# Row sums of the softmax from pairs of key tiles, and an fp16 low-rank product, in a layer of two MoE-LoRA half steps around causal attention

## The chip, the cores and the metric

The kernel runs on one core of a Trainium2 chip. The metric is the device time of one execution in microseconds (us); lower is better. The core has five engines with a queue each, served in order: TensorE (PE, matmuls; its weight loads are listed apart as PEld), VectorE (DVE), ScalarE (ACT), GpSimd (POOL) and SyncE (SP, which here only issues DMAs). Engines wait for each other through semaphores.

## What is computed

```python
x = x + 0.5 * ffn(layernorm(x))
x = x + attention(layernorm(x))
x = x + 0.5 * ffn(layernorm(x))

# ffn: 8 experts, top 2, rank 16
logits = x @ gate_w.T
w      = softmax over the two largest logits, 0 elsewhere
low    = x @ lora_A.T                     # per expert, 8 x 16 = 128 values
y      = x @ base_w.T + base_b + 2.0 * sum over experts of w * (low @ lora_B.T)

# attention: 32 query heads, 8 key-value heads, head size 32, causal, rotary
att   = (q @ k.T) / sqrt(32), masked
probs = softmax(att)
out   = (probs @ v) @ Wo
```

x has 2 x 1024 rows of 1024 values, all in fp32.

## The kernel before, in words

**Tiles.** The 2048 rows are 16 tiles of 128 rows, eight in each of the two batches (TPB = 8). A tile passes four stages: a1 (layernorm, first ffn), a2 (layernorm, keys, values and queries), the attention proper, c1 (output matrix) and c2 (layernorm, second ffn, store). A planner written out by hand (NORMAL, SEQS, plan, step, lines 807 to 939) mixes pieces of the dense stages of later and earlier tiles into the attention units of the current tile. The framework then orders the instructions of each engine by a timeline of its own, so that a change in one place can redraw the order elsewhere.

**Precision.** Large products are made of fp16 halves: each operand is scaled by a power of two (pow2, line 167, which squares and sums the weights on ACT, spreads the largest row sum with a small matmul and takes a power of two from it), a high half is its fp16 rounding and a low half the rest (split, line 195). A dense product is three fp16 matmuls for each 128 of the contraction (lines 361 to 363: high x high, high x low, low x high), 512 columns wide.

**The ffn** (lines 393 to 447). The gate and low-rank products of a tile come first (136 columns); then the eight experts' weights are made on DVE and ACT and multiplied into the 128 low-rank values, with the factor inva2 that undoes the scale of lora_A (line 418). After the base product of each half (512 columns) three more matmuls add the low-rank part into the same PSUM tile (lines 441 to 443). Their operands, lh, ll and lbh, lbl, are halves in fp32r, a form of fp32. lora_B therefore is scaled by the scale of the base weights alone (prep_lora, line 226). L444 then adds the result to x.

**Attention** (lines 556 to 696). A unit is one query tile and one key-value group of four query heads; with L key tiles in reach (1 to 8), there are 128 units and 576 pairs of a unit and a key tile. unit_s1 finds the row maxima: for each key tile four matmuls into one of two PSUM buffers (L568), and a maximum on DVE (L585). Where L > 2, the diagonal tile goes through ACT (L579) and a select on POOL (L580) first. The maxima are written into two spare columns of the queries, which are transposed by a DMA (qt_load, line 549). LOOK lets this run 3 to 6 units ahead. unit_s2 then makes the scores with the key on the partitions (L683, one matmul of 512 columns), and the exponentials on ACT (L689, tile p32, 8 buffers); in the diagonal tile POOL sets what is masked to 0 (L691).

**The weighted sum** (av_batch, line 615). Up to four key tiles (BATCH) of one unit wait in pend, and a batch is issued when two more key tiles (SKEW) have been made. For each key tile, last one first, PE multiplies the exponentials with the values and then with a matrix of ones; the ones product gives the row sums, spread over the 32 rows of a head. Both are fp32 matmuls with 32 columns of weights and 128 columns of data, one for each of the four heads, placed in four column groups of the array. The matmuls of a batch are held in a row. At the end of a unit ACT copies both results out (L637), DVE takes the reciprocal of the sums and multiplies (L639, L644), and ACT and POOL write the fp16 halves for the output product (L645, L646).

**The start** (lines 741 to 799). SP issues the loads in program order while pinned is set: x of tile 0, the gate's and lora_A's weights, two pieces of the base weights, x of tile 1, then two more pieces, lora_B (lst, line 758), x of tile 2. prep_gate, prep_base and prep_lora scale and split them.

Of the kernel before, what the change touches and what calls it, by code (L numbers as in the profile page):

```python
# [9 lines left out]
FP = mybir.dt.float32  # L10
FPR = mybir.dt.float32r
HP = mybir.dt.float16
I32 = mybir.dt.int32
AF = mybir.ActivationFunctionType
ALU = mybir.AluOpType
# [5 lines left out]
P = 128  # L21
# [19 lines left out]
def kernel(  # L41
# [77 lines left out]
    def pin(ins):  # L119

        if pinned[0]:
            tc.keep_in_program_order(ins)
# [12 lines left out]
    ag = wres.tile([P, 2, KB, P + E], HP)  # L135
    lbh = wres.tile([P, D], FPR)
    lbl = wres.tile([P, D], FPR)
    wstr = dram.tile([5, 2, P, 2, KB // 2, 512], HP)
# [27 lines left out]

    def pow2(aps, junk, name):

# [11 lines left out]
        e = small.tile([P, 1], FP, name="e")  # L180
        nc.vector.tensor_scalar(e.bitcast(I32), ar.bitcast(I32), 0x7F800000, None, ALU.bitwise_and)
        tag = "_".join(map(str, name))
        s = const.tile([P, 1], FP, name="s_" + tag)
# [20 lines left out]
    def prep_base(n, sts):  # L204
        pow2(sts, [wb[:, n, 0, h * HK : (h + 1) * HK, :] for h in range(2)], ("b", n))
        for k in range(KB):
            after = (None, None)
            if n == 0 and k > 0:
                after = ("xn", "nb") if k == 1 else ("hi", "lo")
            split(wb[:, n, 0, k, :], wb[:, n, 1, k, :], sts[k // HK][:, k % HK, :], S["b", n], k, after)  # L210
        u = const.tile([P, 1], FP, name=f"uf{n}")
        nc.gpsimd.tensor_scalar(u, INV["b", n], 0.5 / XS, 0.0, ALU.mult, ALU.add)
        S["uf", n] = u

    def prep_gate(sts):
# [6 lines left out]
        inva2 = const.tile([P, 1], FP)  # L222
        nc.gpsimd.tensor_scalar(inva2, INV["a",], 2.0, 0.0, ALU.mult, ALU.add)
        S["cg"], S["inva2"] = cg, inva2
# [168 lines left out]
    def ffn(xt, tt, done):  # L393
# [32 lines left out]
        for n in range(2):  # L426
# [5 lines left out]
            if n == 0:  # L432
                pst = p_misc.tile([P, 512], FP, name="misc")
                nc.tensor.transpose(pst[:, 0:P], lw.rearrange("p e r -> p (e r)"), ident)
                lh = small.tile([P, P], FPR, name="lh", bufs=LB)
                ll = small.tile([P, P], FPR, name="ll", bufs=LB)
                nc.scalar.copy(lh, pst[:, 0:P])
                nc.vector.tensor_tensor(ll, pst[:, 0:P], lh.bitcast(FP), ALU.subtract)
                yield
# [175 lines left out]
    def av_batch():  # L615

        t, g, L, us = pend.popleft()
        if us[0][0] == 0:
            avt[0] = p_av.tile([P, 2, P], FP, name="av")
        av = avt[0]  # L620
        prev = None
        for n, (j, p32) in enumerate(reversed(us)):
            for i, w in enumerate((VA[t - t % TPB + j][:, g, :], ones)):
                for h in range(GRP):
                    rows = slice(h * DH, (h + 1) * DH)
                    with ExitStack() as st:
                        if prev is not None:
                            st.enter_context(tc.high_priority())
                            st.enter_context(tc.issue_after(prev.ins))
                        prev = nc.tensor.matmul(  # L630
                            av[rows, i, :], lhsT=w, rhs=p32[:, h, :],
                            start=(us[0][0] == 0 and n == 0 and i == 0), stop=(us[-1][0] == L - 1 and n == len(us) - 1),
                            skip_group_check=True, tile_position=(0, h * DH),
                        )
        if us[-1][0] == L - 1:
            o = pp.tile([P, 2, P], FP, name="o", bufs=2)
# [12 lines left out]

    def av_add(t, g, j, L, p32):  # L650

        if not pend or len(pend[-1][3]) == BATCH or pend[-1][0:2] != (t, g):
            pend.append((t, g, L, []))
        pend[-1][3].append((j, p32))
        after = 0
# [20 lines left out]
    def unit_s2(t, g):  # L676
# [4 lines left out]
        for j in range(L):  # L681
# [8 lines left out]
            if j == L - 1:  # L690
# [3 lines left out]
                )  # L694
            av_add(t, g, j, L, p32)
            yield
# [46 lines left out]
    for h in range(2):  # L743
        for src, c in ((a_in, slice(0, P)), (g_in, slice(P, P + E))):
# [258 lines left out]
```

## Time and profile before

| | |
|---|---|
| time, median of 3 runs | 1538.43 us (1531.92 to 1540.04) |
| time of the profiled execution | 1540.01 us |
| its span, first to last instruction | 1538.2 us |
| PE busy | 1434.5 us, 93% |
| DVE busy | 1080.9 us, 70% |
| ACT busy | 691.1 us, 45% |
| POOL busy | 480.0 us, 31% |
| row sums' matmuls (L630, ones) busy | 232.1 us |
| low-rank matmuls (L441, L442, L443) busy | 35.7, 25.7 and 26.8 us |
| chain that ended last, PE's share | 70% |

Busy time is the time in which at least one instruction of a group or engine runs; matmuls overlap, so their mean duration is longer than the distance from one to the next. An fp32 matmul leaves two records in the trace. A line such as "PE s L568 <- DVE mx L585" reads: the instruction of line 568, which writes tile s, waited for the one of line 585 on DVE, which writes mx; then come the total in us, the number of times and the longest.

### The profile page before, as it was taken

The page shows a single profiled execution, that of the slowest core. Times are in us where ns is not written, and L with a number is a line of the kernel's source. Part 1 is how long each engine was busy: PE and PEld are TensorE (multiplying, and loading weights), DVE is VectorE, ACT ScalarE, POOL GpSimd, SP SyncE. Part 2 cuts the span into 40 slices and gives each one's busy share as a digit, 9 for nine tenths or more (in the row PEclk, how much of TensorE's full clock was granted, in tenths as well). Part 3 has the DMA queues.
Part 4 walks back from the last instruction along what each step waited for, and adds up shares of the span by engine and source line. Part 5 has one row for each costly group of instructions (what it writes and reads, how often), then busy time and mean ns, then how long its engine had stood idle before and what let it go on. Part 6 is the DMA issues. An engine that isn't in the chain of part 4 may idle for free.

```text
span 1538.2 us, 39420 instructions
## 1 busy us (share of the span) xinstructions
PE 1434.5 (93%) x16594; PEld 846.2 (55%) x16594; DVE 1080.9 (70%) x2382; ACT 691.1 (45%) x1276; POOL 480.0 (31%) x678
## 2 busy tenths in 40 slices
PE   3687889899999999999999998999999999999997
PEld 2333445455656566666654454555656656666543
DVE  5968666958768577777664866867768577776553
ACT  7453334444444454454550334444445445555420
POOL 2544332524324133232131433433333232221221
PEclk9998999999999999999999999999999999999999
DMA  9776797969383763855647769566493753553551
GB/s 301 250 207 185 172 242 190 235 166 242 84 254 96 209 173 79 238 106 146 184 116 244 178 189 257 157 196 203 111 256 75 220 145 97 194 132 96 112 180 42
DMA packets 297186, 267.57 MB, mean 174 GB/s; under 512 B 262576, under 2 KB 265648, under 8 KB 276528
## 3 DMA queue, kind: packets, MB, share of 16 engines
q1 hardware_dynamic: 293456, 252.47, 61.5%
q10 hardware_dynamic: 3552, 12.58, 2.1%
q8 instruction: 130, 2.13, 0.6%
q14 instruction: 48, 0.39, 0.1%
HBM read 181.63 MB, written 20.45 MB: 131 GB/s over the span
## 4 chain that ended last, share of the span: by engine, by line
PE 70%; DVE 11%; DMA 10%; issue 3%; POOL 2%; ACT 2%; SPq 1%; ACTq 0%; DVEq 0%; POOLq 0%
PE av L630 14%; PE pd L361 12%; PE pd L362 12%; PE pd L363 12%; PE s L568 8%; PE s L683 7%; DMA qt<-qst 5%; DMA ws<-wstr 2%; DVE mx L585 2%; DVE hl L314 2%; DMA tt<-hl 2%; DVE rc L639 1%; PE pd L441 1%; PE pd L442 1%; PE pd L443 1%
## 5 line engine op out<-in xcount | busy, mean ns | idle before, releaser
L689 ACT ACTIVATE p<-s,cs 128x512 f32<-128x512 f32 x576 | 380.0, 688 | 279.4 <-PE s L683 276.2
L585 DVE TENSOR_REDUCE mx<-s 128x4 f32<-128x512 f32 x480 | 316.4, 676 | 182.0 <-PE s L568 155.9
L630 PE MATMUL av<-p,va 128*32 128x128 f32 x4608 | 236.6, 277 | 2.3 <-POOL p L691 1.3
L361 PE MATMUL pd<-ws,tt 128*128 128x512 f16 x592 | 225.4, 381 | 13.8 <-DMA ws<-wstr 9.4
L630 PE MATMUL av<-p,ones 128*32 128x128 f32 x4608 | 232.1, 273 | 0.0
L362 PE MATMUL pd<-ws,tt 128*128 128x512 f16 x592 | 225.2, 380 | 0.0
L363 PE MATMUL pd<-ws,tt 128*128 128x512 f16 x592 | 224.6, 380 | 0.0
L361 PEld LDWEIGHTS <-tt 128*128 128x128 f16 x1360 | 134.2, 99 | 163.3 <-DMA tt<-hl 28.1
L568 PE MATMUL s<-kts,qt 96*128 96x128 f16 x2304 | 200.0, 220 | 15.3 <-DMA qt<-qst 10.3
L361 PE MATMUL pd<-wb,tt 128*128 128x512 f16 x512 | 196.1, 383 | 17.2 <-DVE xt L444 11.7
L362 PEld LDWEIGHTS <-tt 128*128 128x128 f16 x1360 | 134.2, 99 | 140.4 <-issue 25.0
L683 PE MATMUL s<-qt,kts 128*128 128x512 f16 x576 | 201.9, 382 | 9.3 <-DMA qt<-qst 7.8
L568 PEld LDWEIGHTS <-qt 96*128 96x128 f16 x2304 | 149.9, 98 | 101.8 <-issue 37.7
L363 PEld LDWEIGHTS <-tt 128*128 128x128 f16 x1360 | 134.1, 99 | 129.3 <-issue 7.0
L362 PE MATMUL pd<-wb,tt 128*128 128x512 f16 x512 | 195.9, 383 | 2.2 <-DVE wb L202 2.2
L363 PE MATMUL pd<-wb,tt 128*128 128x512 f16 x512 | 195.7, 382 | 0.0
L630 PEld LDWEIGHTS av<-p,va 128*32 128x32 f32 x4608 | 122.4, 109 | 66.0 <-issue 54.8
L646 POOL TENSOR_TENSOR tt<-o,tt 128x128 f16<-128x128 f32 x128 | 62.7, 490 | 305.1 <-ACT tt L645 305.1
L691 POOL TENSOR_SCALAR_AFFINE_SELECT p<-p 128x512 f32<-128x512 f32 x128 | 85.9, 672 | 198.2 <-ACT p L689 197.1
L639 DVE RECIPROCAL rc<-o 128x128 f32<-128x128 f32 x128 | 121.0, 945 | 37.2 <-ACT o L637 36.9
L630 PEld LDWEIGHTS av<-p,ones 128*32 128x32 f32 x4608 | 138.2, 110 | 0.1
L580 POOL TENSOR_SCALAR_AFFINE_SELECT sm<-sm 128x512 f32<-128x512 f32 x96 | 67.8, 706 | 216.1 <-ACT sm L579 213.5
(164 smaller groups left out, 1815.6 us busy)
## 6 DMA issues: line engine op xcount, KB each, us to landing
ws<-wstr SPq DMA_DIRECT2D x148, 1024.0 KB, 5.9
wstr<-ws ACTq DMA_DIRECT2D x9, 1024.0 KB, 6.5
xt<-in_x_dram SPq DMA_DIRECT2D x16, 512.0 KB, 3.7
out_dram<-xt SPq DMA_DIRECT2D x15, 512.0 KB, 3.1
qt<-qst SPq DMA_TRANSPOSE x256, 3.0
ws<-in_wb_dram SPq DMA_DIRECT2D x2, 1024.0 KB, 8.4
qst<-in_wb_dram SPq DMA_DIRECT2D x2, 1024.0 KB, 7.9
st<-in_wo_dram SPq DMA_DIRECT2D x2, 1024.0 KB, 11.3
```

The costliest lines, as they stand in the source:

```text
L361: nc.tensor.matmul(ps, lhsT=th, rhs=wh, start=(k == 0), stop=False)
L362: nc.tensor.matmul(ps, lhsT=th, rhs=wl, start=False, stop=False)
L363: nc.tensor.matmul(ps, lhsT=tl, rhs=wh, start=False, stop=(last and k == KB - 1))
L568: nc.tensor.matmul(ps[:, h, :], lhsT=q[0 : 3 * DH, h, :], rhs=KT[b0 + j][0 : 3 * DH, g, :], start=(not pem or h == 0), stop=not pem,)
L580: nc.gpsimd.affine_select(out=sm, in_=sm, compare_op=ALU.is_ge, fill=-3.0e38, base=0, pattern=[[0, GRP], [-1, P]], channel_multiplier=1,)
L585: nc.vector.tensor_reduce(mx[:, j, :], ps, AX.X, ALU.max)
L630: prev = nc.tensor.matmul(av[rows, i, :], lhsT=w, rhs=p32[:, h, :], start=(us[0][0] == 0 and n == 0 and i == 0), stop=(us[-1][0] == L - 1 ...
L639: nc.vector.reciprocal(rc, o[:, 1, :])
L646: nc.gpsimd.tensor_tensor(c.low(g), o2, c.high(g), ALU.subtract)
L683: ins = nc.tensor.matmul(ps.rearrange("p h k -> p (h k)"), lhsT=KT[b0 + j][:, g, :], rhs=q.rearrange("p h k -> p (h k)"), start=True, stop ...
L689: nc.scalar.activation(p32, ps, AF.Exp, scale=cs)
L691: nc.gpsimd.affine_select(out=p32, in_=p32, compare_op=ALU.is_ge, fill=0.0, base=0, pattern=[[0, GRP], [1, P]], channel_multiplier=-1,)
```

## The change

Two parts.

First, the row sums: when a unit has made an odd-numbered key tile's exponentials, DVE adds them to those of the tile before (128x512, fp32, a new tile "pair" with 3 buffers), and PE multiplies the sum with ones, once for the pair. A last tile without a partner is multiplied by itself. In a batch, the value products of all its tiles come first and the ones products after them.

Second, the low-rank product: lbh, lbl, lh and ll become fp16. lora_B gets a power-of-two scale of its own, so it is loaded ahead of the base weights, and its sum of squares is taken right after the gate's. The scales of the base weights get a lower bound ("least"), inva2 is put together from three scales once the first base scale is known, and the factors of lora_B's two halves are made in prep_lora.

```diff
-    lbh = wres.tile([P, D], FPR)
-    lbl = wres.tile([P, D], FPR)
+    lbh = wres.tile([P, D], HP)
+    lbl = wres.tile([P, D], HP)
...
-    def pow2(aps, junk, name):
+    def pow2(aps, junk, name, least=None):
...
+        if least is not None:
+            nc.vector.tensor_tensor(e, e, least, ALU.max)
...
     def prep_base(n, sts):
-        pow2(sts, [wb[:, n, 0, h * HK : (h + 1) * HK, :] for h in range(2)], ("b", n))
+
+        least = const.tile([P, 1], FP, name=f"lb{n}")
+        if n == 0:
+            nc.vector.scalar_tensor_tensor(least, INV["a",], 2.0**32, INV["l",], ALU.mult, ALU.mult)
+        else:
+            nc.vector.tensor_scalar(least, INV["b", 0], 16384.0, None, ALU.mult)
+        pow2(sts, [wb[:, n, 0, h * HK : (h + 1) * HK, :] for h in range(2)], ("b", n), least)
+        if n == 0:
+            inva2 = const.tile([P, 1], FP)
+            nc.vector.scalar_tensor_tensor(inva2, INV["a",], 2.0, INV["l",], ALU.mult, ALU.mult)
+            nc.vector.tensor_tensor(inva2, inva2, S["b", 0], ALU.mult)
+            S["inva2"] = inva2
...
     def prep_lora(st):
+        c = const.tile([P, 2], FP, name="sl")
+        nc.vector.tensor_copy(c[:, 0:1], S["l",])
+        nc.vector.scalar_tensor_tensor(c[:, 1:2], INV["b", 0], S["l",], S["b", 1], ALU.mult, ALU.mult)
         for n in range(2):
-            c = bass.ts(n, 512)
-            nc.scalar.activation(lbh[:, c], st[:, c], AF.Copy, scale=S["b", n])
-            nc.vector.scalar_tensor_tensor(
-                lbl[:, c], st[:, c], S["b", n], lbh[:, c].bitcast(FP), ALU.mult, ALU.subtract
-            )
+            h, s = bass.ts(n, 512), c[:, n : n + 1]
+            nc.scalar.activation(lbh[:, h], st[:, h], AF.Copy, scale=s)
+            nc.vector.scalar_tensor_tensor(lbl[:, h], st[:, h], s, lbh[:, h], ALU.mult, ALU.subtract)
...
-                lh = small.tile([P, P], FPR, name="lh", bufs=LB)
-                ll = small.tile([P, P], FPR, name="ll", bufs=LB)
+                lh = small.tile([P, P], HP, name="lh", bufs=LB)
+                ll = small.tile([P, P], HP, name="ll", bufs=LB)
...
-        for n, (j, p32) in enumerate(reversed(us)):
-            for i, w in enumerate((VA[t - t % TPB + j][:, g, :], ones)):
-                for h in range(GRP):
...
+        last = us[-1][0] == L - 1
+        runs = [(0, VA[t - t % TPB + j][:, g, :], p32) for j, p32, _ in reversed(us)]
+        runs += [(1, ones, sums) for _, _, sums in reversed(us) if sums is not None]
         prev = None
+        for n, (i, w, p32) in enumerate(runs):
+            for h in range(GRP):
...
-            av_add(t, g, j, L, p32)
+            sums = None
+            if j % 2 == 1:
+                sums = pp.tile([P, GRP, P], FP, name="pair", bufs=3)
+                nc.vector.tensor_tensor(sums, even, p32, ALU.add)
+            elif j == L - 1:
+                sums = p32
+            even = p32
+            av_add(t, g, j, L, p32, sums)
             yield
...
+    lst = xp.tile([P, D], FP, name="xt")
+    pin(nc.sync.dma_start(out=lst, in_=lb_in))
     b0 = [piece(h - 2, [wb_in[:, 0:512]], h, nc.sync) for h in range(2)]
...
     prep_gate(gst)
+    pow2([lst[:, bass.ts(h, 512)] for h in range(2)], [lbh[:, bass.ts(h, 512)] for h in range(2)], ("l",))
     b1 = [piece(3 + h, [wb_in[:, 512:1024]], h, nc.sync) for h in range(2)]
-    lst = xp.tile([P, D], FP, name="xt")
-    pin(nc.sync.dma_start(out=lst, in_=lb_in))
```

More of the change, by code (lines that the diff above doesn't have):

```diff
@@ L10 @@
 FP = mybir.dt.float32
-FPR = mybir.dt.float32r
 HP = mybir.dt.float16
@@ L221, in prep_gate @@
         nc.gpsimd.tensor_scalar(cg, INV["a",], 1.0 / XS, 0.0, ALU.mult, ALU.add)
-        inva2 = const.tile([P, 1], FP)
-        nc.gpsimd.tensor_scalar(inva2, INV["a",], 2.0, 0.0, ALU.mult, ALU.add)
-        S["cg"], S["inva2"] = cg, inva2
+        S["cg"] = cg
     def prep_lora(st):
+        c = const.tile([P, 2], FP, name="sl")
+        nc.vector.tensor_copy(c[:, 0:1], S["l",])
+        nc.vector.scalar_tensor_tensor(c[:, 1:2], INV["b", 0], S["l",], S["b", 1], ALU.mult, ALU.mult)
         for n in range(2):
-            c = bass.ts(n, 512)
-            nc.scalar.activation(lbh[:, c], st[:, c], AF.Copy, scale=S["b", n])
-            nc.vector.scalar_tensor_tensor(
-                lbl[:, c], st[:, c], S["b", n], lbh[:, c].bitcast(FP), ALU.mult, ALU.subtract
-            )
+            h, s = bass.ts(n, 512), c[:, n : n + 1]
+            nc.scalar.activation(lbh[:, h], st[:, h], AF.Copy, scale=s)
+            nc.vector.scalar_tensor_tensor(lbl[:, h], st[:, h], s, lbh[:, h], ALU.mult, ALU.subtract)
         nc.scalar.mul(bb, bb, 0.5)
@@ L434, in ffn @@
                 nc.tensor.transpose(pst[:, 0:P], lw.rearrange("p e r -> p (e r)"), ident)
-                lh = small.tile([P, P], FPR, name="lh", bufs=LB)
-                ll = small.tile([P, P], FPR, name="ll", bufs=LB)
+                lh = small.tile([P, P], HP, name="lh", bufs=LB)
+                ll = small.tile([P, P], HP, name="ll", bufs=LB)
                 nc.scalar.copy(lh, pst[:, 0:P])
-                nc.vector.tensor_tensor(ll, pst[:, 0:P], lh.bitcast(FP), ALU.subtract)
+                nc.vector.tensor_tensor(ll, pst[:, 0:P], lh, ALU.subtract)
                 yield
@@ L620, in av_batch @@
         av = avt[0]
+        last = us[-1][0] == L - 1
+        runs = [(0, VA[t - t % TPB + j][:, g, :], p32) for j, p32, _ in reversed(us)]
+        runs += [(1, ones, sums) for _, _, sums in reversed(us) if sums is not None]
         prev = None
-        for n, (j, p32) in enumerate(reversed(us)):
-            for i, w in enumerate((VA[t - t % TPB + j][:, g, :], ones)):
-                for h in range(GRP):
[L625 to L635, printed above, removed]
+        for n, (i, w, p32) in enumerate(runs):
+            for h in range(GRP):
+                rows = slice(h * DH, (h + 1) * DH)
+                with ExitStack() as st:
+                    if prev is not None:
+                        st.enter_context(tc.high_priority())
+                        st.enter_context(tc.issue_after(prev.ins))
+                    prev = nc.tensor.matmul(
+                        av[rows, i, :], lhsT=w, rhs=p32[:, h, :],
+                        start=(us[0][0] == 0 and n == 0), stop=(last and n == len(runs) - 1),
+                        skip_group_check=True, tile_position=(0, h * DH),
+                    )
+        if last:
             o = pp.tile([P, 2, P], FP, name="o", bufs=2)
@@ L648, in av_batch, with av_add @@
                 CT[t] = CTX.pop(t)
-    def av_add(t, g, j, L, p32):
+    def av_add(t, g, j, L, p32, sums):
         if not pend or len(pend[-1][3]) == BATCH or pend[-1][0:2] != (t, g):
             pend.append((t, g, L, []))
-        pend[-1][3].append((j, p32))
+        pend[-1][3].append((j, p32, sums))
         after = 0
```

## The prediction

> **What bounds the kernel now.** I read the page's 40 slices first, then a table of windows, then the list of waits, the chain of work that ended last, and the groups of instructions by line.
>
> ```profile
> PE   3687889899999999999999998999999999999997
> DVE  5968666958768577777664866867768577776553
> ```
>
> TensorE (PE) is above 90% in nearly every slice from the tenth on, VectorE (DVE) at 6 to 8 tenths. Before about 300 us PE has holes; they belong to the preparation of the weights. The windows give the middle (stretch, length, then busy us and instructions of PE, its weight loads, DVE, ScalarE = ACT, GpSimd = POOL; clock, DMA share, GB/s):
>
> ```profile
> 300.00:400.00 100.00, 97.08 (x1188) 59.80 (x1188) 74.06 (x179) 47.01 (x94) 30.78 (x49) 1.00 0.72 176
> 400.00:500.00 100.00, 100.00 (x1235) 60.19 (x1233) 75.18 (x157) 46.36 (x86) 35.81 (x46) 1.00 0.59 163
> 600.00:700.00 100.00, 99.69 (x1355) 62.29 (x1355) 71.95 (x151) 49.71 (x90) 27.44 (x38) 1.00 0.62 161
> 1000.00:1100.00 100.00, 98.13 (x1115) 58.16 (x1113) 75.63 (x160) 45.31 (x86) 36.65 (x48) 1.00 0.61 168
> 1300.00:1400.00 100.00, 97.32 (x1501) 63.13 (x1500) 74.67 (x146) 56.30 (x102) 23.67 (x37) 1.00 0.58 172
> ```
>
> PE is full at full clock, and in the whole run it waits 2.8 us for DVE's row maxima, the one place in attention where DVE could hold it often:
>
> ```profile
> PE s L568 <- DVE mx L585: 2.8, 6, 0.8
> ```
>
> So a microsecond taken from PE in the middle is one off the time, as long as DVE can carry what it is given.
>
> **Ones products (L630).** The chain shows whole batches of the weighted sum (start, length, what):
>
> ```profile
> 592.23 1.88 PE av L630 x64
> 599.97 1.45 PE av L630 x48
> ```
>
> The trace holds 9,216 matmul records on this line for 4,608 that the program issues, two for each in fp32. A key tile is 4 heads x (values + ones) x 2 = 16 records, so these are batches of four tiles and of three, and one tile costs 1.88 - 1.45 = 0.43 us (0.436 by the unrounded starts). The groups by line split it evenly (values busy 236.6 us, ones 232.1), so the ones product of one tile (four heads) is 0.218 us. A unit of L key tiles now needs ceil(L/2) of them instead of L: over L = 1 to 8 that is 20 for 36, times 8 key-value groups and 2 batches 320 for 576. **256 x 0.218 = 55.8 us** leave PE, all where it is full (the attention runs from 168 to 1500 us).
>
> **Pair sums on DVE.** 256 adds of 128x512 in fp32, two SBUF inputs, are new. The same operation stands in the trace as the rotary sum, L483 (min/median/max of both its sizes):
>
> ```profile
> L483 DVE TENSOR_TENSOR t<-t,t x48: 418/692/1172, 99.7 to 1356.4; 128x512 f32<-128x512 f32 x32, 128x256 f32<-128x256 f32 x16
> ```
>
> In the page's costliest groups, the maxima:
>
> ```profile
> L585 DVE TENSOR_REDUCE mx<-s 128x4 f32<-128x512 f32 x480 | 316.4, 676 | 182.0 <-PE s L568 155.9
> ```
>
> Its 32 large ones have a mean of 749 ns: 689 where POOL is idle, 907 where POOL runs through all of it. Two L585 in a row take 1.19 to 1.20 us in the chain, not 2 x 0.676 = 1.35, so about 0.08 of each lies under the next. I take 0.749 - 0.08 = 0.67 us; the bounds are 0.60 (two in a row, no POOL) and 0.91. That is 172 us more DVE work, from 1081 to about 1253 us: in a run of 1490 us, 84% on average. Placed by stage: exponentials (L689, one per key tile) lie 43, 42, 53, 40 and 66 to the windows shown, and 0.444 pairs come on each tile. DVE then needs 87, 88, 88, 88 and 94 us, while PE (less 0.097 us per tile, and 0.6 for the next item) needs 92, 95, 94, 94 and 90. Only the last window has DVE above PE, by 4 us; the others lie at 92 to 94% of PE's time. That is more than the trace shows DVE to carry without loss: its fullest 50 us beside a full PE are 42.8 (350 to 400 us), 86%. Above this a late reduction of maxima (behind a 0.95 us reciprocal, an add, or a subtraction L314 of up to 3.4 us) reaches PE, since the scores have two PSUM buffers. From 0 upwards I take 1 us for each of the eight other windows of 100 us with 40 key tiles or more, and 4 for the last: **+12 us**. Zero holds if the lookahead of 3 to 6 units absorbs all of it; the upper bound is in the second rival.
>
> [...] L314, of the same kind with 1024 elements, goes from 1159 to 3387 ns, and its long ones lie beside POOL work:
>
> ```profile
> L314 DVE TENSOR_TENSOR hl<-xn,hl x48: 1159/1643/3387, 11.8 to 1511.4; 128x1024 f16<-128x1024 f32 x48
> ```
>
> [...] The sum goes by the measured means.
>
> **New wait of PE for the sum.** The ones products now stand behind the value products of their batch. Where the pair ends in the diagonal tile (64 of 256), DVE waits for POOL's select, then adds (0.69 us), while PE still has 2 to 4 value products (0.44 to 0.87 us). Batches are issued two key tiles late, and POOL's select holds L630 for 1.3 us (its weight loads for 4.5) in the whole run, so most sums are ready long before. On DVE the maxima stand behind that wait. I count it in the 12. ACT's exponentials have 8 buffers as before, and the sums 3, of which a batch uses two.
>
> **fp16 low-rank product.** Three fp32 products of 512 columns per half tile, 64 times (mean 559, 402 and 424 ns, overlapping). Inside the full stretch:
>
> ```profile
> 788.56 0.61 PE L683 MATMUL s<-qt,kts 128*128 128x512 f16 x2
> 788.82 0.58 PE L441 MATMUL pd<-lbh,lh 128*128 128x512 f32 x1
> 789.24 0.40 PE L442 MATMUL pd<-lbl,lh 128*128 128x512 f32 x1
> 789.47 0.39 PE L443 MATMUL pd<-lbh,ll 128*128 128x512 f32 x1
> ```
>
> From the end before them (789.17) to their last end (789.86) are 0.69 us, 0.23 each; fp16 products of that size repeat at 0.216 in the chain. That and the slower start of the product behind give 0.053 x 64 = **3.4 us**. Weight loads of 192 ns become 99, beneath matmuls. Bounds 0 and 15 (all of 559 + 402 + 424 - 3 x 382 = 239 ns).
>
> **Preparation.** lora_B's 512 KB now go ahead of the base weights on SP's queue: 1.7 us at the 305 GB/s of the first 40 us, for all that follows there (two base pieces, x1). ACT does two more squares ahead of those of the base weights (L171, 128x544: 0.65 each, 1.3 us), with ten small operations on DVE and POOL and a product on PE, which lie under the base load. The gate's products stand behind the scale of the base weights on PE; they took 17.5 to 20.6 us, and PE then idled 4.9 us until 25.8, which covers them. Load and squares overlap: **+2 us**, bounds -2 (the whole order of the first 300 us, where PE idles some 70 us, is drawn anew) and +6. inva2 now needs the base scale, which is there before L418 reads it.
>
> **Sum** on the profiled execution: span 1538.2 - 55.8 - 3.4 + 2 + 12 = 1493.0, plus the 1.8 us around it (its time is 1540.0) = 1494.8. The median of the three runs is 1.6 below that execution: **1493 us**.
>
> **Rivals.**
> 1. *DVE never decides.* For it: 2.8 us of waiting now, and no window but one where DVE needs more than PE. Against it: 92 to 94% with a queue in order. The sum without the 12: 1481 us (1474 to 1486).
> 2. *DVE becomes the bound.* At 0.91 us an add the five windows ask 91, 92, 93, 92 and 101 us of DVE: 1 to 3 under PE, and 11 over it in the last. With 3 us lost in each of eight windows and 11 in the last, 35 in place of 12: 1516 us (1507 to 1531). For it: POOL's selects run just where the adds do. Against it: the mean of L483 is 749.
> 3. *Slower.* One mechanism: in the 64 diagonal pairs DVE, in order, stands until POOL's select is done, itself behind POOL's L396 (2.44 us); maxima and buffers stop, and PE after them. To eat the 57 us gained and 8 more (0.5%) each must cost PE 1.0 us, the point from which it decides; 2.44 + 0.67 less a cover of some 2 us is 1.1: 1481 + 70 = 1551 us. Against it speaks that two key tiles (over 4 us) lie between exponential and batch.
> 4. *No change:* waits of 0.8 us at those 64 places, 1538. That the ones are not saved is excluded by the program as built: 1,280 such products for 2,304, 256 adds.
>
> **How the numbers follow.** Forecast (1486 to 1507) 0.42; first rival 0.25; second 0.20; fourth 0.06; third 0.05; lower than all, by the redrawn preparation, 0.02. The range takes the forecast, the first rival and most of the second: 1472 to 1522. Faster by over 0.5% (7.7 us, about what a measurement here can tell from no change): 0.89; within 0.06; slower 0.05.
>
> **What would show it.** Right: the ones group near 130 us busy, PE still above 95% in the middle, DVE 82 to 86% of the span, adds of 700 to 800 ns, PE's waits for DVE (maxima, pair sums) between 8 and 25 us. First rival: these under 5. Second: over 30, with DVE above 95% in windows and PE below 93. Third: a DVE wait for L691 of tens of us. Wrong from the start: an offset of over 6 us already at the first exponential (162.8 us now).

## The result, and the profile after

The changed kernel takes **1563.91 us** (median of 4 runs, 1561.90 to 1565.74) against 1537.22 us for the kernel before in the same comparison: a ratio of **1.0159 [1.0139, 1.0180]**, slower by some 24 us (the two medians taken alone differ by 27). The forecast was 1493 us with a range of 1472 to 1522; the time lies outside it, and on the other side.

The page of the changed kernel begins with the engines' busy time and, in its 40 slices, PE, DVE and the granted clock:

```profile
PE 1413.8 (90%) x14548; PEld 788.9 (50%) x14548; DVE 1230.2 (79%) x2652; ACT 690.2 (44%) x1280; POOL 507.4 (32%) x679
...
PE   3689788799999998999989998999999999989888
...
DVE  6978567878979789888775778788979898898753
...
PEclk9889989989999999999989999999999999999999
```

PE has 2,046 records fewer, and yet its busy time fell only from 1434.5 to 1413.8 us, 20.7 and not 56. Its idle time (span less busy) rose from 103.7 to 150.1, by 46.4. 46.4 - 20.7 = 25.7 is the whole difference of the spans, 1563.9 - 1538.2. So there are two questions: why PE stands still more, and why less work keeps it busy nearly as long.

The five windows that the prediction showed, now (stretch, length, busy us and instructions of PE, weight loads, DVE, ACT, POOL; clock, DMA share, GB/s):

```profile
300.00:400.00 100.00, 90.64 (x971) 53.48 (x970) 83.21 (x174) 45.18 (x91) 37.58 (x49) 0.91 0.69 184
400.00:500.00 100.00, 97.31 (x1089) 55.73 (x1086) 87.16 (x186) 46.17 (x89) 34.37 (x48) 1.00 0.55 159
600.00:700.00 100.00, 95.65 (x1123) 55.69 (x1126) 85.04 (x167) 47.97 (x85) 27.62 (x34) 0.98 0.58 156
1000.00:1100.00 100.00, 92.55 (x963) 53.07 (x962) 86.90 (x187) 44.51 (x86) 35.32 (x49) 0.98 0.68 177
1300.00:1400.00 100.00, 92.10 (x1257) 56.21 (x1256) 86.08 (x164) 52.45 (x96) 23.66 (x35) 1.00 0.56 158
```

PE was 97 to 100% busy here; now it has 3 to 9% of holes, and three of the five stretches show a granted clock below 1.00, where all five had 1.00. DVE stands at 83 to 87%, not full. The chain of work that ended last says the same by engine, before and then after:

```profile
PE 70%; DVE 11%; DMA 10%; issue 3%; POOL 2%; ACT 2%; SPq 1%; ACTq 0%; DVEq 0%; POOLq 0%
```

```profile
PE 49%; DVE 26%; DMA 12%; issue 5%; POOL 3%; ACT 3%; SPq 0%; ACTq 0%; POOLq 0%; DVEq 0%
```

PE's waits by what ended them (total, times, longest), before:

```profile
PE s L568 <- DMA qt<-qst: 10.3, 7, 3.2
...
PE s L683 <- DMA qt<-qst: 7.8, 6, 1.9
...
PE av L630 <- POOL p L691: 1.3, 2, 1.0
```

And after:

```profile
PE s L696 <- DMA qt<-qst: 25.8, 25, 2.8
PE s L579 <- DVE mx L596: 16.4, 27, 2.2
...
PE pd L372 <- DMA ws<-wstr: 12.4, 8, 3.9
PE av L643 <- POOL p L704: 9.7, 8, 5.3
...
PE s L579 <- DMA qt<-qst: 4.1, 3, 2.0
...
PE av L643 <- DVE pair L711: 3.5, 6, 1.2
```

The waits for the maxima rose from 2.8 to 16.4 us, those for POOL's select of the diagonal tile (L704, before L691) from 1.3 to 9.7, those for the transposed queries from 18.1 to 29.9 (L696, before L683, from 7.8 to 25.8; L579, before L568, fell from 10.3 to 4.1). DVE writes the source of that transpose (qst, L606 and L607), so a late DVE can stand behind a wait that bears the DMA's name. The trace fits this without proving it: of the 22 such waits over 0.3 us behind 150 us, 17 belong to a DMA issued within 0.4 us of DVE's last write, and in 18 DVE had been busy for over 90% of the 5 us before that write, against 68% of all 128 such writes. The sums themselves are hardly waited for: 3.5 us.

Where is the time lost? I counted the exponentials on ACT (one per key tile): the first starts at 162.0 us (before 162.8), the 49th at 334.3 (314.2), the 169th at 603.6 (585.0), the 288th at 832.9 (805.4), the last at 1511.6 (1483.0). The start costs nothing; 21 us are lost in the first 48 key tiles, and behind them 528 key tiles bring 8 more, where a gain of about 50 was forecast. (The trace of e2, an experiment below without any add, has its 49th at 321.1, so 7 of the 21 are not the adds'.)

The longest gap shows how such a delay comes about. First it by windows, then by instructions (start, length, engine, line):

```profile
288.40:302.00 13.60, 13.59 (x146) 7.62 (x145) 11.09 (x22) 7.15 (x12) 11.64 (x13) 1.00 1.03 302
302.00:305.40 3.40, 0.60 (x5) 0.27 (x5) 3.37 (x5) 2.32 (x5) 3.40 (x3) 0.99 0.89 330
305.40:322.50 17.10, 10.83 (x110) 7.40 (x114) 13.72 (x27) 6.06 (x12) 7.11 (x10) 0.50 0.49 126
322.50:340.00 17.50, 17.31 (x195) 10.07 (x188) 13.79 (x36) 8.25 (x18) 3.36 (x7) 1.00 0.18 37
```

```profile
301.16 2.78 POOL L407 TENSOR_TENSOR xt<-xt,bb 128x1024 f32<-128x1024 f32 x1
...
302.44 2.04 DVE L711 TENSOR_TENSOR pair<-p,p 128x512 f32<-128x512 f32 x1
...
303.63 0.69 ACT L702 ACTIVATE p<-s,cs 128x512 f32<-128x512 f32 x1
...
304.73 1.69 POOL L591 TENSOR_SCALAR_AFFINE_SELECT sm<-sm 128x512 f32<-128x512 f32 x1
...
308.24 0.63 POOL L704 TENSOR_SCALAR_AFFINE_SELECT p<-p 128x512 f32<-128x512 f32 x1
...
308.93 0.44 PE L643 MATMUL av<-p,va 128*32 128x128 f32 x4 [5.33 <-POOL p L704]
```

From 302.0 to 305.4 DVE and POOL are both full and PE does 0.60 us of work. A pair sum takes 2.04 us there instead of 0.68, beside POOL's bias add. The exponential that PE needs next is done at 304.3, but its select stands in POOL's queue until 308.24; PE waits 5.33 us. So what ends this gap is POOL's queue, with DVE's as full beside it. It is not the usual case: of the 29 gaps over 1.2 us between 150 and 1530 us, 13 end with a transposed query, 4 with a maximum and 2 with POOL's select.

**And then the clock is 0.50 for 17.1 us.** In a row, the next matmul starts 426 ns after an L696 at half clock instead of 220, and 107 ns after an L579 instead of 56 (medians of the whole trace). PE is busy for 10.83 of the 17.1 us, so about half of that, some 5 us, comes on top of the gap. The trace of after has 107 us at half clock, before 51. (1 - mean clock) x span, 0.034 x 1563.9 = 53 us against 0.016 x 1538.2 = 25 us, is an upper bound of what that costs, since PE is idle for part of it: PE is busy for 81 us of the half-clock time in after and for 34 before. Half of each, 41 and 17 us, makes an estimate of 24 us for the slower clock, out of the 35 by which PE's busy time misses the forecast.

### The profile page after: what moved, and what is told of

Its sections match the earlier page's. It is cut to its first block, busy times and chain, and to the rows that moved or that the text cites. A ratio compares the mean times of both kernels' runs of the same rounds, so it can differ in the third digit from the quotient of the medians.

```text
span 1563.9 us, 35637 instructions
## 1 busy us (share of the span) xinstructions
PE 1413.8 (90%) x14548; PEld 788.9 (50%) x14548; DVE 1230.2 (79%) x2652; ACT 690.2 (44%) x1280; POOL 507.4 (32%) x679
## 4 chain that ended last, share of the span: by engine, by line
PE 49%; DVE 26%; DMA 12%; issue 5%; POOL 3%; ACT 3%; SPq 0%; ACTq 0%; POOLq 0%; DVEq 0%
PE pd L372 10%; PE pd L373 9%; PE pd L374 9%; PE av L643 7%; DMA qt<-qst 6%; DVE mx L596 6%; PE s L696 5%; PE s L579 5%; DVE hl L325 3%; DMA ws<-wstr 3%; DVE pair L711 3%; DVE rc L652 2%; DMA tt<-hl 2%; DVE ws L203 2%; DVE bst L345 1%
## 5 line engine op out<-in xcount | busy, mean ns | idle before, releaser
L579 PE MATMUL s<-kts,qt 96*128 96x128 f16 x2304 | 208.3, 222 | 26.5 <-DVE mx L596 16.4
L696 PE MATMUL s<-qt,kts 128*128 128x512 f16 x576 | 205.5, 390 | 28.6 <-DMA qt<-qst 25.8
L711 DVE TENSOR_TENSOR pair<-p,p 128x512 f32<-128x512 f32 x256 | 187.9, 735 | 38.1 <-ACT p L702 30.0
L579 PEld LDWEIGHTS <-qt 96*128 96x128 f16 x2304 | 156.6, 98 | 117.8 <-issue 54.5
L372 PEld LDWEIGHTS <-tt 128*128 128x128 f16 x1360 | 136.1, 100 | 150.0 <-DMA tt<-hl 17.7
L373 PEld LDWEIGHTS <-tt 128*128 128x128 f16 x1360 | 136.3, 100 | 144.8 <-issue 28.7
L372 PE MATMUL pd<-wb,tt 128*128 128x512 f16 x512 | 198.0, 387 | 10.2 <-DMA tt<-hl 4.2
L374 PEld LDWEIGHTS <-tt 128*128 128x128 f16 x1360 | 136.1, 100 | 131.9 <-issue 12.1
L643 PE MATMUL av<-p,va 128*32 128x128 f32 x4608 | 167.5, 279 | 12.0 <-POOL p L704 9.7
L659 POOL TENSOR_TENSOR tt<-o,tt 128x128 f16<-128x128 f32 x128 | 69.2, 541 | 301.3 <-ACT tt L658 301.2
L704 POOL TENSOR_SCALAR_AFFINE_SELECT p<-p 128x512 f32<-128x512 f32 x128 | 90.0, 704 | 224.0 <-ACT p L702 214.9
L643 PEld LDWEIGHTS av<-p,va 128*32 128x32 f32 x4608 | 115.4, 110 | 72.3 <-issue 49.6
L591 POOL TENSOR_SCALAR_AFFINE_SELECT sm<-sm 128x512 f32<-128x512 f32 x96 | 74.1, 772 | 194.3 <-ACT sm L590 184.5
L325 DVE TENSOR_TENSOR hl<-xn,hl 128x1024 f16<-128x1024 f32 x48 | 94.3, 1965 | 14.0 <-POOL hl L324 13.9
```

Of the source, the lines that this page charges most:

```text
L325: marks["lo"] = nc.vector.tensor_tensor(self.hl[:, (2 * i + 1) * w : (2 * i + 2) * w], src, hi, ALU.subtract)
L372: nc.tensor.matmul(ps, lhsT=th, rhs=wh, start=(k == 0), stop=False)
L373: nc.tensor.matmul(ps, lhsT=th, rhs=wl, start=False, stop=False)
L374: nc.tensor.matmul(ps, lhsT=tl, rhs=wh, start=False, stop=(last and k == KB - 1))
L579: nc.tensor.matmul(ps[:, h, :], lhsT=q[0 : 3 * DH, h, :], rhs=KT[b0 + j][0 : 3 * DH, g, :], start=(not pem or h == 0), stop=not pem,)
L643: prev = nc.tensor.matmul(av[rows, i, :], lhsT=w, rhs=p32[:, h, :], start=(us[0][0] == 0 and n == 0), stop=(last and n == len(runs) - 1), ...
```

## The experiments

Medians of the kernel before differ by up to 6 us between the comparisons (1537 to 1543), so differences between experiments are taken from the ratios, each to its own runs of the kernel before, and 1% is 15.4 us. The intervals are about 0.2% to each side, 3 us. "After" stands at 1.0159. The main theory (Q in the expectations): DVE, in order and full for stretches of ten microseconds, delivers late; each delay leaves PE idle, and gaps bring the half clock. The rivals: the fp16 part (P) or the order within a batch (B) costs the time; the redrawn order of the instructions does (R); the place of the adds does; POOL's select in the diagonal pairs does.

### The two parts, and the adds by themselves

**e2_fp16_only**: the low-rank part and the start as after, the attention as before.

> The changed kernel with its attention part as before (a ones product for every key tile, no pair sums); only the fp16 low-rank product and the new order of the start remain. Theory Q (the adds crowd DVE's queue, and maxima and query transposes come late): this part is not the cause, 1530 to 1540 us against 1537 before. Rival P (the cost lies in the fp16 part and the redrawn start): 1590 to 1620 us, for the 56 us that the ones products were to save must then have been saved, and 26 us were lost on top; anything above 1555 speaks for P. Rival R (each redraw of the order by the framework moves the time by itself): anywhere from 1520 to 1560.

Measured 1542.72 us, 1.0019 [1.0003, 1.0036]: the fp16 part gains nothing and costs little. PE is busy 1438.4 us.

**e10_order_only**: e2 with the values of a batch first and the ones products last, one for each tile as before.

```diff
-        for n, (j, p32) in enumerate(reversed(us)):
-            for i, w in enumerate((VA[t - t % TPB + j][:, g, :], ones)):
+        for i in range(2):
+            for n, (j, p32) in enumerate(reversed(us)):
+                w = (VA[t - t % TPB + j][:, g, :], ones)[i]
```

> The fp16-only kernel (1543 us) with the new order inside a batch: all value products first, then all ones products; no pairs, no adds. Without the adds the change had won 34 of the 56 us that the ones products cost. If the order (values first, so that the diagonal tile's select is needed earlier than its ones product would be) took the missing 20: 1555 to 1565. If these 20 are transfers and transposes that a faster PE now meets: 1539 to 1547.

Measured 1542.76 us, 1.0009 [0.9992, 1.0025]. Without pairs the order is free.

**e4_no_adds**: after without the sums; the ones products multiply the odd tile of a pair alone, so the even tile's row sum is left out (and 1 is added as the result is copied out).

```diff
-                sums = pp.tile([P, GRP, P], FP, name="pair", bufs=3)
-                nc.vector.tensor_tensor(sums, even, p32, ALU.add)
+                sums = p32
```

> The changed kernel without the adds: for each pair the ones product takes the exponentials of the odd tile alone, so the row sums leave out every even tile that has a partner, and 1 is added to both results as ACT copies them out, to keep the quotient finite. PE's work and the order inside a batch are those of the change. Theory Q: the whole gain appears, 1475 to 1490 us, and PE is over 97% busy from 300 to 800 us. Rival B (values first and ones last in a batch, with the wait for POOL's select): it stays above 1540. Rival R: anything between.

Measured 1508.93 us, 0.9789 [0.9766, 0.9812]. PE and its waits:

```profile
PE 1384.0 (92%) x14548; PEld 781.8 (52%) x14548; DVE 1079.4 (72%) x2396; ACT 693.5 (46%) x1280; POOL 491.8 (33%) x679
```

```profile
PE pd L372 <- DMA ws<-wstr: 16.3, 13, 3.6
...
PE s L696 <- DMA qt<-qst: 14.9, 13, 3.1
...
PE s L579 <- DMA qt<-qst: 9.0, 9, 3.6
PE s L579 <- DVE mx L596: 7.5, 17, 0.9
```

Against e2 PE is busy 1438.4 - 1384.0 = 54.4 us less: the saving that the prediction worked out. But the time falls by 2.30%, 35 us, and 1475 to 1490 us was missed. Some 19 us do not appear; PE's idle time is 124.0 us against 100.5 in e2. A shorter PE finds the weights (ws), the transposes (qt: 11.1 us in e2, 23.9 here) and the maxima not yet there, though no add was made.

**e3_adds_only**: e2 with the 256 adds, whose sums nobody multiplies; the ones products are those of before.

> As the fp16-only kernel, and DVE makes the 256 pair sums, but nobody multiplies them: PE still makes all 576 ones products. Theory Q: the price of the adds alone; the change lost 26 us where 57 were to be won, so 83 us if the price is the same beside a fuller PE, 1600 to 1620; with PE less idle between some of it is hidden, at least 1560. Rival R and the rival that the new order inside a batch is the cause (B): the same as the fp16-only kernel within 10 us.

Measured 1577.03 us, 1.0238 [1.0222, 1.0253]: 34 us for adds that no engine waits for, since their result is not used. What they cost is DVE's time, not the wait for the sum. Nor do they hold up ACT by keeping the exponentials' buffers: ACT's exponentials (p) wait for no add, neither here nor in after. And from e4 to after the same adds cost 3.70%, 57 us, on a PE that has less to do. About half of that is idle time (124.0 to 150.1 us): PE waits 8.9 us more for the maxima, 6.0 for the transposed queries, 4.2 for POOL's select and 3.5 for the sums. The other half is the same matmuls made longer (busy 1384.0 to 1413.8). The clock is an estimated 17 of these 30 us (PE is busy at half clock for 81 us against 47, of which half is counted); the other 12 or so are not explained.

**e6_half_adds**: the adds for two of four heads (128x256, 470 ns each, 120 us in all); the other two heads multiply the odd tile alone, which leaves part of their sums out.

```diff
-                nc.vector.tensor_tensor(sums, even, p32, ALU.add)
+                nc.vector.tensor_tensor(sums[:, 0:2, :], even[:, 0:2, :], p32[:, 0:2, :], ALU.add)
```

> The changed kernel with adds of half the width: the pair sum is made for two of the four heads (128x256), the other two heads multiply the odd tile alone, so their row sums leave out the even tiles (1 is added to both results as they are copied out, as in the kernel without adds). PE's work and the number of adds and of waits are those of the change; DVE's time for the adds is about 256 x 0.43 = 110 us in place of 188. If the price follows DVE's time (theory Q): between the 1509 without adds and the 1564 with them, 1509 + 55 x 110/188 = 1541, within 8. If it follows the number of waits and places in the queue: 1555 to 1564. If a threshold of load is what counts: 1510 to 1525.

```profile
L712 DVE TENSOR_TENSOR pair<-p,p 128x256 f32<-128x256 f32 x256 | 120.1, 470 | 38.3 <-ACT p L703 33.5 <-POOL p L705 4.0 <-issue 0.4
```

Measured 1529.62 us, 0.9927 [0.9906, 0.9948], between the range for a price by DVE's time (1533 to 1549) and the one for a threshold of load (1510 to 1525). With 0, 120 and 188 us of adds the kernel stands at 0.9789, 0.9927 and 1.0159: the first 120 cost 21 us, the next 68 cost 36. The price of a microsecond on DVE rises from 0.18 to 0.53. That excludes a fixed price for an add, since their number is the same, and fits a queue that fills.

### Does the place matter, or DVE's time wherever it is spent?

**e9_later**: each add is issued one key tile later, when both exponentials have long been done.

> The changed kernel with each pair sum issued one key tile later, so that a maximum due at the same time goes first and the sum of a diagonal pair waits less for POOL's select. If the place of the adds ahead of the maxima is what hurts: 1535 to 1550. If it is DVE's time as such: 1558 to 1570, and PE may wait longer for the sums (3.5 us now).

**e7_look**: the maxima run a unit further ahead (LOOK [6, 6, 5, 5, 4, 4, 4, 4], six buffers for the transposed queries; pair has two).

> The changed kernel with the maxima one unit further ahead from the third key tile on (LOOK 6, 6, 5, 5, 4, 4, 4, 4), six buffers for the transposed queries and two for the pair sums. Theory Q says that PE stalls because maxima, and behind them the transposes of the queries, come late by a few us; a unit more of lead then covers the DMA waits of the scores (26 us and 4 us in the change) but not the maxima's own two PSUM buffers (16 us): 1530 to 1548 us, and fewer half-clock spells. If DVE is short of time altogether, lead doesn't help: 1558 to 1570.

Measured 1567.09 us, 1.0168 [1.0134, 1.0202], and 1572.65 us, 1.0216 [1.0187, 1.0246]. Neither gains. That speaks against the place of the adds and fits a queue that has too much in it: later adds and an earlier start of the maxima only move it. In e7 the sums have a buffer less, and PE's waits for them rose from 3.5 to 5.8 us, which could hide a gain of about 2 us.

**e17_no_adds_look**: e4 (and what it leaves out) with the same lead, to see whether the 19 us that e4 misses are a lack of lead.

> The kernel without adds (1509 us, even tiles left out of the row sums) with one unit more lead for the maxima (LOOK 6, 6, 5, 5, 4, 4, 4, 4) and six buffers for the transposed queries. If the 20 us that the saved products did not bring are lost because query transposes and maxima come too late for a faster PE: 1485 to 1500. If they are lost elsewhere (weight loads, half clock after gaps, the redrawn order): 1504 to 1515.

Measured 1513.34 us, 0.9800 [0.9767, 0.9833]: no gain. These 19 us stay open.

**e13_no_reciprocal** and **e14_before_no_reciprocal**: after and before without the division by the row sums (a constant tile takes the reciprocal's place). That takes 128 x 0.944 = 121 us of work from DVE in a place that has nothing to do with pairs.

```diff
-            nc.vector.reciprocal(rc, o[:, 1, :])
...
-            nc.vector.tensor_tensor(o2, o[:, 0, :], rc, ALU.mult)
+            nc.vector.tensor_tensor(o2, o[:, 0, :], fixed, ALU.mult)
```

> The changed kernel without the reciprocals: the weighted sums are multiplied by a constant tile, so the division by the row sums is left out. It takes 121 us from DVE at a place that has nothing to do with the adds; PE's work, the adds, their order and their waits stay. Theory Q in its present form (DVE is full for stretches of 10 us and more, so its time counts, wherever it is spent): from 1564 to 1505 to 1530 us, as if most of the adds' 188 us were gone. If the adds hurt by their own waits or their place: above 1550.

> The kernel before, also without the reciprocals (same edit, division left out). Theory Q: DVE didn't bind there, so 121 us less of DVE change little, 1525 to 1540. If less DVE work helps every kernel alike: 1500 to 1515, and the run before this one says nothing of the adds.

Measured 1525.51 us, 0.9898 [0.9878, 0.9918], and 1540.12 us, 1.0007 [0.9987, 1.0026]. This pair carries the theory: the same edit brings 40 us in the changed kernel (0.33 for each microsecond of DVE) and nothing in the kernel before. DVE's time is free before (within some 3 us), and it has a price after. The pages of e13 and then of e14:

```profile
PE 1397.5 (92%) x14548; PEld 783.1 (51%) x14548; DVE 1144.2 (75%) x2524; ACT 688.8 (45%) x1280; POOL 507.5 (33%) x680
```

```profile
PE 1437.1 (93%) x16594; PEld 847.0 (55%) x16594; DVE 993.7 (65%) x2254; ACT 687.2 (45%) x1276; POOL 489.5 (32%) x679
```

DVE's busy time fell by 86 and 87 us only, since other instructions took longer (the layernorm's subtraction 2.28 us in e13, 1.97 in after); by busy time the price is 0.47. POOL's busy time is that of after (507.5 and 507.4), so POOL's load does not explain these 40 us.

Why the averages don't show it: after 300 us I cut the traces into stretches of 10 us and counted those with DVE busy for 95% or more: 7 before, 27 after (17 in e13, 20 in e6). With other places of the cuts it is 4 to 7, 25 to 36, 12 to 18 and 15 to 21. Of PE's gaps over 0.3 us between 300 us and the last exponential, those that follow 10 us with DVE over 90% busy make 3.4 of 22.0 us before and 34.0 of 61.7 after. The count does not rank the kernels by itself: e18, e15, e8 and e20 below have 19 to 23 such stretches on average and lie at 1.0196, 0.9832, 1.0030 and 0.9965.

### The adds on another engine

**e5_pool_adds**: the adds on GpSimd.

```diff
-                nc.vector.tensor_tensor(sums, even, p32, ALU.add)
+                nc.gpsimd.tensor_tensor(sums, even, p32, ALU.add)
```

> The changed kernel with its 256 pair sums on GpSimd instead of DVE. L396, the same operation on twice the elements, takes 2.44 us there, so one sum should take some 1.2 us, 310 us in all on top of 480: 52% of the span. Theory Q: DVE is as free as before, so 1490 to 1520 us, less than the full gain because POOL's selects now stand behind sums and DVE's two-input operations run beside more POOL work. Rival B: above 1550. If any two-input sum beside the other engine is what hurts: 1560 or more, with long L314 and long sums.

Measured 1563.78 us, 1.0166 [1.0127, 1.0205], no better, where the main theory had 1490 to 1520.

```profile
L711 POOL TENSOR_TENSOR pair<-p,p 128x512 f32<-128x512 f32 x256 | 341.1, 1334 | 193.9 <-ACT p L702 188.6
```

An add takes 1.33 us there against 0.735 on DVE, POOL's busy time goes to 824.0 us, and DVE, with the adds gone, is busy 1176.4 us against 1079.4 in e4, with the same instructions: the adds on POOL cost DVE 97 us of stretching.

**e12_pool_pow**: after with the reciprocal on GpSimd, as a power of -1.

> The changed kernel with the reciprocals on GpSimd, as a power of -1. GpSimd's power of one element takes 0.55 to 0.59 us and a plain operation on 128 elements 0.49 us; if the power of 128 elements is below 2 us, GpSimd stays under 50% and DVE loses 121 us, and theory Q gives 1510 to 1540, with luck below the kernel before. If the power takes 4 us or more, GpSimd is over 1,000 us and its selects come late: slower than the change.

Measured 3303.16 us, 2.1444 [2.1409, 2.1480]: one power of 128x128 takes 20.8 us there, 2,665 us in all. Nothing follows for the question.

### Which adds are dear

**e8_diag_alone**: the diagonal tile gets no partner, so that no add stands behind POOL's select: 192 adds and 1,536 ones matmuls in place of 256 and 1,280.

```diff
-            if j % 2 == 1:
+            if j % 2 == 1 and j < L - 1:
...
+            if j == L - 1 and j % 2 == 1:
+                pend[-1][3][-1] = (j - 1, even, even)
```

> The changed kernel in which the diagonal tile has no partner: 192 adds in place of 256 and 1,536 ones products in place of 1,280, and no sum waits for POOL's select. By the prices found so far (55 us for 256 adds, 34 us won by 256 products): 1564 - 14 + 8 = 1558, within 8. If DVE standing still for POOL's select is a good part of the loss: 1530 to 1545.

**e18_diag_kept**: the same counts the other way round: all 64 diagonal pairs are kept, and in the units with 3, 4, 6 and 8 key tiles the two tiles of the first pair, 64 pairs that never hold a diagonal tile, are multiplied by ones one by one.

```diff
+            skip = L in (3, 4, 6, 8) and j < 2
+            if skip:
+                sums = p32
-            if j % 2 == 1:
+            elif j % 2 == 1:
```

> The changed kernel with as many adds and ones products as the one with the diagonal tiles alone (192 and 1,536), but the 64 pairs given up are others: the first pair of the units of 3, 4, 6 and 8 key tiles. All 64 diagonal pairs, whose sums stand behind POOL's select in DVE's queue, are kept. If the wait for the select is worth some 14 us: 1554 to 1564. If only the load counts: 1540 to 1549, as the kernel with the diagonal tiles alone (1544).

Measured 1543.97 us, 1.0030 [1.0017, 1.0043], and 1572.99 us, 1.0196 [1.0163, 1.0228]: 26 us apart with equal counts. PE and its waits for the sums in e8, then in e18:

```profile
PE 1406.8 (92%) x15060; PEld 799.4 (52%) x15060; DVE 1192.9 (78%) x2588; ACT 690.5 (45%) x1280; POOL 505.6 (33%) x679
```

```profile
PE av L643 <- DVE pair L711: 0.4, 1, 0.4
```

```profile
PE 1424.8 (91%) x15060; PEld 798.9 (51%) x15060; DVE 1198.9 (76%) x2588; ACT 691.3 (44%) x1280; POOL 505.9 (32%) x679
```

```profile
PE av L643 <- DVE pair L714: 6.0, 7, 1.4
```

The same number of matmuls keeps PE busy 18.0 us longer in e18, an estimated 13 of it by the clock (76 against 103 us at half speed, PE busy in 54 and 80 of them). PE's waits for the sums are only 6 us in e18; that the diagonal sums act in the main through the clock and through what stands behind them on DVE is an inference. Against after, leaving out 64 diagonal adds brings 20 us, leaving out 64 others brings nothing (6 us more), which was not expected. How much of the 26 us is a redrawn order of the instructions can't be told: edits that should cost nothing moved after by up to 9 us (e7, e9).

### Relief for DVE and POOL

**e20_high_on_act**: after, with the high fp16 halves of every layernorm on ACT instead of GpSimd (the code did so for the first two tiles already). It takes no instruction from DVE, but the work on POOL beside it.

```diff
-    def layernorm(xt, act=False, n=1):
+    def layernorm(xt, act=True, n=1):
...
-        tt = layernorm(xts[t], t < 2)
+        tt = layernorm(xts[t])
```

> The changed kernel with only the high halves of the layernorm outputs on ScalarE; DVE keeps its copies. GpSimd loses 49 us in 46 pieces of 1.08 us, which stand in its queue ahead of selects and beside DVE's two-input operations; DVE's own work is the same but for the stretching of L325 (1.97 us a piece against 1.54). If GpSimd's queue and the collisions are the larger part: 1517 to 1533. If DVE's 18 us of copies are: 1545 to 1562.

**e15_act_relief**: that, and the copies of the high halves of keys and queries on ACT instead of DVE.

```diff
-        nc.vector.tensor_copy(ks[:, :, 2 * DH : 3 * DH], ks[:, :, 0:DH])
+        nc.scalar.copy(ks[:, :, 2 * DH : 3 * DH], ks[:, :, 0:DH])
...
-        nc.vector.tensor_copy(qs[:, h, DH : 2 * DH], qs[:, h, 0:DH])
+        nc.scalar.copy(qs[:, h, DH : 2 * DH], qs[:, h, 0:DH])
```

> The changed kernel, whole, with work of other stages taken off DVE and GpSimd: the high half of each layernorm output is made on ScalarE instead of GpSimd (so that the subtraction after it, L325, with a mean of 1.97 us, runs beside less GpSimd work), and the copies of the high halves of queries and keys (18 us) go from DVE to ScalarE. DVE should lose 18 us and some 30 us of stretching; at the 0.31 us per us that the run without reciprocals showed: 1564 - 15 = 1549, within 10. If only the adds' own place counts: 1560 or more.

**e16_diag_alone_relief**: e8 with the relief of e15.

> The same relief on the kernel with the diagonal tiles alone (1544 us), the whole computation. By theory Q: 1522 to 1537, so at last below the kernel before (1540). If DVE is no longer what binds there: 1540 to 1548.

**e19_before_relief**: the kernel before with the relief of e15, as a control.

> The kernel before with the same relief (high halves of the layernorm outputs and the copies of the high halves on ScalarE). If DVE and GpSimd bind only through the pair sums: 1532 to 1543, no change, as without the reciprocals. If the relief helps every kernel: 1490 to 1520, and the changed kernel with it (1517) owes nothing to the pairs.

| | median us | ratio | PE busy | DVE busy | half clock, us |
|---|---|---|---|---|---|
| after | 1563.91 | 1.0159 [1.0139, 1.0180] | 1413.8 | 1230.2 | 107 |
| e20 | 1534.65 | 0.9965 [0.9944, 0.9985] | 1401.4 | 1195.3 | 78 |
| e15 | 1517.13 | 0.9832 [0.9799, 0.9865] | 1397.8 | 1185.3 | 71 |
| e16 | **1512.97** | **0.9798 [0.9767, 0.9829]** | 1395.1 | 1156.3 | 47 |
| e19 | 1535.39 | 0.9973 [0.9958, 0.9988] | 1433.9 | 1032.4 | 52 |

The three columns on the right are of one execution each, which lies up to 5 us from the median (e15: 1522.48; e20: 1530.82).

The relief is worth 50 us in the changed kernel (1.0159 to 0.9832) and 4 in the kernel before. So most of its value is not its own: it pays back what the adds took. Not all of it does. Counting as lost PE's idle time and half of its busy time at half clock, PE has lost 61 us in after by 180 us, where no kernel of the table has made an add; in e20 it is 55, in e15 53, in e16 52. Over the whole run it is 191, 159, 151 and 135. So 6 to 9 us of the relief belong to the start; whether they come with the fp16 part's new start was not tried (e2 with the relief). With the relief the pairs do bring something: e15 is 22 us below e19, and e16, ahead of both the kernel before and the changed one, 27 us; 7 and 8 of these lie ahead of the first add (e19 has lost 61 by then). I had expected far less of e15 and e16, and somewhat more of e20. The subtraction on DVE that follows those high halves, in after and in e20 (min/median/max):

```profile
L325 DVE TENSOR_TENSOR hl<-xn,hl x48: 1161/1442/3393, 14.7 to 1536.9; 128x1024 f16<-128x1024 f32 x48
```

```profile
L325 DVE TENSOR_TENSOR hl<-xn,hl x48: 1202/1226/3247, 14.5 to 1504.9; 128x1024 f16<-128x1024 f32 x48
```

e20 moves no instruction off DVE and yet takes 35 us from its busy time: with POOL busy 453.8 in place of 507.4 us, less of DVE's work is stretched. A window (1000 to 1100 us) of e16 that was among the worst in after:

```profile
1000.00:1100.00 100.00, 96.96 (x1096) 56.41 (x1095) 78.45 (x170) 49.38 (x94) 31.24 (x43) 1.00 0.68 194
```

PE is at 97% and full clock again, with DVE at 78 instead of 87.

## Why the prediction was wrong, point by point

- **Ones products, -55.8 us.** Right as work: e4 shows 54.4. As time it is 35. "A microsecond taken from PE in the middle is one off the time" failed: 0.65 of each came through, with DVE no busier than in e2 (1079.4 against 1091.0 us). The condition put to it, that DVE can carry its load, was too narrow: in e4 PE waits more for weights and transposes too.
- **The adds' duration, 0.749 us.** Right: mean 735 ns (634/681/2045).

```profile
L711 DVE TENSOR_TENSOR pair<-p,p 128x512 f32<-128x512 f32 x256 | 187.9, 735 | 38.1 <-ACT p L702 30.0 <-POOL p L704 7.4
```

  By the means of L483, (749 - 689) x 256 = 15 us of it are stretching beside POOL; measured are (735 - 681) x 256 = 14 us, with 681 ns the mean of the 146 adds beside an idle POOL. (The bound of 907 ns "where POOL runs through all of it" was the mean of three sums only, one of them 692; the 24 adds wholly beside POOL took 937.) In the gap shown above, the add began at 302.44, POOL's bias add ended at 303.94, and the sum was there 0.54 us later.
- **DVE's waits, +12 us: this step failed.** "1 us for each of the eight other windows of 100 us ... and 4 for the last" compares averages over 100 us, and found DVE at 92 to 94% of PE's time. The adds cost 57 us from e4 to after. A queue in order is full in stretches of ten microseconds (27 of them for 7), as where a layernorm's subtraction, a rotary sum and a select come together in the gap shown; that the lookahead runs out there is an inference, and a longer one (e7) brought nothing. The term had no part for the clock, an estimated 17 us of the price, and none for POOL's queue, whose selects DVE and PE stand behind.
- **fp16 low rank, -3.4 us, and preparation, +2 us.** Together +2.9 us measured (e2). The three groups are busy 73.1 us against 88.2 before, but PE's total did not fall. The first exponential, 0.8 us earlier, shows that the start cost nothing.
- **The sum** as measured: -54.4 (ones) + 19.0 (gaps without adds) + 56.9 (adds) + 2.9 (the rest) = +24.4 us, for -45.2 forecast.
- **The rivals.** The second named the mechanism, DVE as the bound, but priced it at 35 us where the adds cost 57, and took the whole saving for granted. The third had the right place, diagonal pairs behind POOL's queue, and its end (1551) was on the right side, at a chance of 0.05; but its price came from a wait of about 1 us of PE in each of 64 pairs, and PE's waits for the sums are 3.5 us in all; DVE's own wait for the select, its sign, is 7.4 us and not tens. The fp16 rivals and the order are excluded by e2 and e10.
- **The signs.** Adds of 700 to 800 ns: right. Ones near 130 us busy: 114. DVE at 82 to 86%: 79. PE above 95% in the middle: two of five windows fell to 92 and one to 91. PE's waits for DVE between 8 and 25: 16.4 + 3.5, inside the band that was to say "right", while the kernel was slower. This sign misled: the waits for transposes (18.1 to 29.9 us) and for the select (1.3 to 9.7) rose too, and the time at half clock (51 to 107), and a late DVE can stand behind these.

Shown by runs: that the adds' time on DVE costs 34 to 57 us; that it rises faster than in proportion; that DVE's time has a price in the changed kernel alone; that the relief pays most of it back. Argued, from the waits and one traced gap: the chain from queue to gap to clock. Open: what holds e4's 19 us, how much of the 26 us between e8 and e18 belongs to the diagonal, and why POOL's relief (e20, 30 us, some 6 of them ahead of the first add) is worth more than the 35 us of DVE time it frees would be at 0.33. POOL's shorter queue may be the rest; no run separates it from DVE's.

## What to carry to other kernels

Before work is moved from a full engine to one that is busy for 70%, look at short stretches, here ten microseconds, and count how many are already full: averages over 100 us hid them. Price the clock too: here PE's gaps came with 107 us at half clock in place of 51, an estimated 24 us for the slower clock. And when the receiving engine gets short of time, give away what others can do (here ACT at 44%) in the same step; on its own that looks worthless, 4 us, and with the change it was worth 50.

## What the runs showed of the hardware

- **The clock.** In after, each of the 13 half-clock spells behind 150 us (before the end of the run) follows a stretch of 3.41 us, as long as the shortest spell, in which PE was idle for 1.5 to 2.9 us. Only two of the gaps around them, 5.33 and 3.89 us, are longer than such a stretch; in the other eleven cases the longest single gap is 1.2 to 3.0 us. Spells last 3.4, 6.8, 10.2 or 17.1 us. So gaps shorter than a stretch, one or several in it, came ahead of most of these spells. They did not always bring one: six other stretches at that spacing, with 1.6 to 2.0 us of idle, were not followed by half clock.
- **DVE beside POOL.** Two-input adds on POOL (e5) raised DVE's busy time by 97 us with the same instructions (1079.4 in e4 to 1176.4), and less work on POOL (e20) lowered it by 35 (1230.2 to 1195.3).
- **GpSimd's power**: 20.8 us for 128 elements in each partition, against 0.94 us for DVE's reciprocal of the same tile.
